# Two groups of 32 nodes, each in half of TensorE's columns, in a graph-attention kernel

## The chip, the cores and the metric

The kernel runs on one core of a Trainium2 chip. The metric is the device time of one execution in microseconds (us). Engines are named as in the profile: PE is TensorE's matmul stream, PEld its weight loads, DVE is VectorE, ACT is ScalarE, POOL is GpSimd and SP is SyncE; a "q" behind a name (SPq) is that engine's instruction queue, which issues transfers.

## The reference

The input is a graph of 6250 nodes with 128 features each and 106250 edges, sorted by destination. Two transformer convolutions with two heads run one after the other, with a batch norm and a ReLU between them, then a residual and a layer norm. All is float32. Cut to what matters:

```
def conv(h, edge_attr, src, dst, W...):          # H = 2 heads, C = 64
    q, k, v = h @ Wq + bq, h @ Wk + bk, h @ Wv + bv
    e = edge_attr @ We                           # edge_attr: 32 cosines of time, 64 given
    alpha = sum_c(q[dst] * (k[src] + e)) / sqrt(C)      # one score for each edge and head
    a = softmax of alpha over the edges of one dst
    return segment_sum((v[src] + e) * a, dst) + h @ Ws + bs
h = relu(batch_norm(conv1(x)))
out = layer_norm(x + conv2(h))
```

## The kernel before

**Plan.** The edges are cut into NC = 106 chunks of whole destination nodes, about 1003 edges and at most NN = 64 nodes each. A chunk occupies CE = 1024 slots: T = 8 blocks of 128 edges, each block a tile with the edges on the partitions. A short stage (`tile_gnn_resnorm`) reads where the chunks begin (`nbs` the first node, `sls` the first edge), turns the edges' sources, destinations and times into columns (`columns`, into `srcs`, `dsts`, `ew`), and tests that the graph fits the scheme. The number of violations ends in `bad`, and the flag `oki` decides at run time between `ordered`, the code below, and `general`, a fallback. Every engine reads `oki`; on SyncE the last of the writes of the feature table `xv_d` stand behind that read.

**Tables.** For each node and head, the query is multiplied into the key matrix beforehand (`tables`), so that the score of an edge is a dot product of a row of the table `tab` with the features of the edge's source, plus one with the edge's own attributes. A code of the node number (`fcode` against bits in the edge's record) adds a huge value where the edge does not belong to the node. So one chunk's scores are a matrix of 128 rows (64 nodes x 2 heads) by 1024 slots, in which only the edges of a row's own node count.

**Rounds.** `conv` runs once for each convolution, over rounds k; each round works on several chunks in a pipeline, in an order written out by hand (`tc.manual_schedule()`):

- `fetch(k + 4)` and `gather(k + 4)`: attributes and table rows come by SyncE's transfers, the features of the edges' sources by eight indirect transfers of 128 rows from GpSimd (L748). Six chunk buffers `ff` are in rotation; one comes free when its chunk's sums are done.
- `score(k, 0)` and `score(k, 1)` (L817, L818): for each half of 512 slots two matmuls, of the source features `ft` and of the edge attributes `et`, into `fps`, two banks of PSUM. Between the halves stands `turn_weights(k - 1)`.
- `lowest(k)` and `weigh(k)` (L823, L830): the minimum of each row on VectorE, the exponent on ScalarE, both over 1024 columns.
- `turn_weights(k - 1)` (L840, L841): the weights are transposed in eight blocks of 128 and copied to `fpt` by ScalarE.
- `turn_in(k + 1, u)` (L797, L806, L801, L807): features and, in the first convolution, attributes of the next chunk are transposed for the scores; ScalarE copies them to `fft` and `fet`.
- `divide`, `finish_turn`, `apply`, `finish` of chunk k - 2 (L852 to L895): the sums are divided by the sum of weights, transposed (`fat`) and multiplied by the value matrix. In the second convolution `apply` has a stationary operand of 64 columns (L883, L884).
- `extra` work, one or two steps in a round: tables of later nodes (L627) and rows of the result.
- `gather_sums(k - 1)` (L847), last in the round: eight matmuls, one for each block, whose stationary operand is a block of the transposed weights (128 slots x 128 rows) and whose moving operand is 225 columns of the block's features and attributes. They add up in one bank, `fpa`.

TensorE takes its instructions in the program's order, so the order above is that of its work. In the trace each float32 matmul of the program is two instructions with a weight load each (848 instructions for 424 calls of L817); a transpose is one.

Of the kernel before, what the change touches and what calls it, by code (L numbers as in the profile page):

```python
# [22 lines left out]
GE = GT * P  # L23
# [21 lines left out]
T = 8  # L45
CE = T * P
NN = P // H
NC = 106
EW = ED + 1

BITS = 8
EC = ED + 2 * BITS
# [482 lines left out]
def room(nc, pl, const, c, w):  # L535
# [38 lines left out]
def matrices(nc, pl, c, const, bank):  # L574
# [3 lines left out]
    for i, w in enumerate((wq, wk, web)):  # L578
# [82 lines left out]
def ordered(ctx: ExitStack, tc: tile.TileContext, pl, x, dst, edge_attr_64, conv2, bn_g, bn_b, out):  # L661


    nc = tc.nc
    N = x.shape[0]
    E = dst.shape[0]
    NP = pl.NP
    hT = pl.hT
    ident, wv, web, tw, tb = pl.ident, pl.wv, pl.web, pl.tw, pl.tb
# [18 lines left out]
    base = N - 2 * NN  # L688
# [10 lines left out]
    def conv(c, extra, first_blocks=None):  # L699
# [4 lines left out]
        work = cs.enter_context(tc.tile_pool(name=f"fwork{c}", bufs=2))  # L704
# [3 lines left out]
        p_s = cs.enter_context(tc.tile_pool(name=f"fp_s{c}", bufs=1, space=bass.MemoryType.PSUM))  # L708
# [10 lines left out]
        def fetch(k):  # L719
# [88 lines left out]
            if u:  # L808
                nc.sync.dma_start(et_d[k], s.et)

        def score(k, u):

            s = ch[k]
            if u == 0:
                s.ps = p_s.tile([P, CE], F32, name="fps")
            w = slice(u * GE, (u + 1) * GE)
            nc.tensor.matmul(s.ps[:, w], s.tab[:, :, 0], s.ft[:, w], start=True, stop=False)  # L817
            nc.tensor.matmul(s.ps[:, w], s.tab[:EC, :, 1], s.et[:, w], start=False, stop=True)  # L818

        def lowest(k):  # L820
            s = ch[k]
            low = small.tile([P, 1], F32, name="flow")
            nc.vector.tensor_reduce(low, s.ps, AX.X, OP.min)  # L823
            s.bias = small.tile([P, 1], F32, name="fm")
            nc.vector.tensor_scalar(s.bias, low, HIGHEST, None, op0=OP.min)  # L825

        def weigh(k):
            s = ch[k]
            s.s = work.tile([P, CE], F32, name="fs")
            nc.scalar.activation(s.s, s.ps, AF.Exp, bias=s.bias, scale=-1.0)  # L830

        def turn_weights(k):

            s = ch[k]
            s.pt = work.tile([P, CE], F32, name="fpt")
            for u in range(2):
                pp = p_tr.tile([P, GE], F32, name="fppt", tag="tr")
                for t in range(4):
                    at = u * GE + t * P
                    nc.tensor.transpose(pp[:, t * P:(t + 1) * P], s.s[:, at:at + P], ident)  # L840
                nc.scalar.copy(s.pt[:, u * GE:(u + 1) * GE], pp)  # L841

        def gather_sums(k):
            s = ch[k]
            s.pa = p_a.tile([P, D + EW], F32, name="fpa")
            for t in range(T):
                nc.tensor.matmul(s.pa, s.pt[:, t * P:(t + 1) * P], s.f[:, t, 1:1 + D + EW], start=t == 0, stop=t == T - 1)  # L847

        def divide(k):
            s = ch[k]  # L850
# [80 lines left out]
        with cs, tc.manual_schedule():  # L931
            for k in range(-AHEAD, NC + 3):
                def on(j):
                    return 0 <= j < NC

                if on(k + AHEAD):
                    fetch(k + AHEAD)
                    gather(k + AHEAD)
                if k == -AHEAD and c:
                    first_blocks()  # L940
                if on(k):
                    score(k, 0)
                if on(k - 1):
                    turn_weights(k - 1)
                place()
                if on(k - 2):
                    divide(k - 2)
                if on(k):
                    score(k, 1)
                if on(k - 2):  # L950
                    finish_turn(k - 2)
                if on(k):
                    lowest(k)
                if on(k + 1):
                    turn_in(k + 1, 0)
                if on(k - 2):
                    apply(k - 2)
                if on(k):
                    weigh(k)
                if on(k + 1):  # L960
                    turn_in(k + 1, 1)
                if on(k - 2):
                    finish(k - 2)
                for j in (k + 2,) if k < SINGLE else (k + 2, k + 3) if k == SINGLE else (k + 3,):
                    if c == 0 and on(j):
                        encode(j)
                        if j < SINGLE + 3:
                            sine()
                if k >= 0:
                    at_round[0] = k  # L970
                    pull(extra, 2 if k < 4 or k > 96 else 1)
                if len(args) == 3 or args and k == NC - 4:
                    sine()
                if c and on(k):
                    if k < RAW:
                        normalise(k)
                    nc.vector.tensor_copy(ch[k].f[:, :, 1 + D:1 + D + TD], ch[k].z)
                for _ in range(min(len(done), 2 if k > NC - 12 else 1)):
# [12 lines left out]
    with tc.tile_pool(name="fpw", bufs=2) as pw:  # L991
# [62 lines left out]
        scale = pl.scale = const.tile([P, 1], F32, name="fscale")  # L1054
# [68 lines left out]
def tile_gnn_resnorm(ctx: ExitStack, tc: tile.TileContext, x, src, dst, edge_attr_64, edge_weight, node_vec,  # L1123
                     time_w, time_b, conv1, conv2, bn_g, bn_b, out):
    nc = tc.nc
    N = x.shape[0]
    E = src.shape[0]
    step = -(-E // NC)
    keep = ctx.enter_context(tc.tile_pool(name="keep", bufs=1))
    made = ctx.enter_context(tc.tile_pool(name="made", bufs=1, space=bass.MemoryType.DRAM))  # L1130

# [5 lines left out]
    with tc.tile_pool(name="plan", bufs=1) as pl, tc.tile_pool(name="planw", bufs=2) as mw, \  # L1137
            tc.tile_pool(name="planp", bufs=2, space=bass.MemoryType.PSUM) as pp, tc.manual_schedule():
        R = NC - 1
        win = pl.tile([R, P], I32, name="win")  # L1140
        for r0, r1 in ((0, R // 16 * 16), (R // 16 * 16, R)):
            nc.sync.dma_start(win[r0:r1], bass.AP(tensor=dst.tensor, offset=dst.offset + step * (r0 + 1) - (P - 1),
                                                  ap=[[step, r1 - r0], [1, P]]))
        NP = got.NP = -(-(N + NN) // GE) * GE
        got.hT = keep.tile([P, NP], F32, name="fhT")
# [19 lines left out]
        jpp = pl.tile([P, P], I32, name="fjp")  # L1165
        nc.gpsimd.iota(jpp, pattern=[[1, P]], base=0, channel_multiplier=-1)
        tau_i = pl.tile([P, 1], I32, name="tau_i")
        nc.gpsimd.iota(tau_i, pattern=[[0, 1]], base=step, channel_multiplier=step)
        lane_i = pl.tile([P, 1], I32, name="lane_i")
        nc.gpsimd.iota(lane_i, pattern=[[0, 1]], base=0, channel_multiplier=1)  # L1170
        ident = got.ident = keep.tile([P, P], F32, name="fident")
# [5 lines left out]
        ends = pl.tile([1, 2, NC + 1], F32, name="ends")  # L1177
# [55 lines left out]
        bad = pl.tile([1, 4], F32, name="bad")  # L1233
        nc.vector.tensor_scalar(bad[:, 3:], ends[:, 0, NC - 2:NC - 1], N - NN + 0.5, None, op0=OP.is_gt)
        nc.vector.tensor_reduce(bad[:, 0:1], span, AX.XY, OP.add)

        two = pl.tile([1, NC - 1], F32, name="two")
# [49 lines left out]
        pb = pp.tile([1, 1], F32, name="pb", tag="one", bufs=1)  # L1287
        nc.tensor.matmul(pb, worst, ones[:, 0:1], start=True, stop=True)
        nc.vector.tensor_copy(bad[:, 1:2], pb)
        tot = pl.tile([1, 1], F32, name="tot")  # L1290
        nc.vector.tensor_reduce(tot, bad, AX.X, OP.add)
        nc.vector.tensor_scalar(oki, tot, 0.0, None, op0=OP.is_equal)
        columns(flats[1], dsts)
        columns(flats[2], ew)

    got.nbs, got.sls = nbs, sls
# [36 lines left out]
```

## Time and profile before

| | |
|---|---|
| median of 14 runs | 2283.13 us (2282.22 to 2286.94) |
| the profiled execution | 2286.03 us |
| its span | 2284.2 us |
| mean granted clock of TensorE | 0.985 |
| first convolution's gathers, first to last start | 37.4 to 1129.0 us |
| second convolution's gathers, first to last start | 1180.6 to 2245.9 us |
| DMA | 396.59 MB, mean 174 GB/s |

The profile is of one execution. Each line of a group shows source line, engine, operation and tiles (written <- read), partitions x elements, the number of instructions, their busy time and mean duration, and the idle time of the engine just ahead of them with what ended it ("issue" where the profile shows no other cause). A timeline line is start, duration, engine, line, operation, and in brackets the idle time before it. The chain of waits is followed back from the last instruction of the program, and its durations reach from one link to the next. Matmuls overlap in the array and their ends are modelled, so for TensorE the distance between starts says more than the durations.

### The profile page before, as it was taken

The numbers are of one execution on the slowest core, as the hardware profiler recorded it, in microseconds if no ns is written. First come the engines' busy times: TensorE is split into PE (matmuls) and PEld (weight loads), VectorE is DVE, ScalarE is ACT, GpSimd is POOL, SyncE is SP. The second block draws the span as 40 slices with busy tenths as digits, with TensorE's granted clock in tenths as the row PEclk, the third lists the DMA queues.
The fourth block names the chain that finished last, engine by engine and source line by source line (L and its number), as shares of the span: only waits on it lengthen the run. The fifth ranks groups of instructions, "written<-read, shape, count | busy, mean of one in ns | idle before, by whom it ended". The sixth has DMA issues, their size and how long they took to land.

```text
span 2284.2 us, 39277 instructions
## 1 busy us (share of the span) xinstructions
PE 2204.6 (97%) x11586; PEld 1705.0 (75%) x11586; DVE 1228.1 (54%) x3738; ACT 1225.4 (54%) x1955; POOL 1623.9 (71%) x1717
## 2 busy tenths in 40 slices
PE   5999999999999999999978999999999999999997
PEld 3687888778787888888855777777777777777775
DVE  5576767676676667777735433333433343433333
ACT  3677777766566666555643344444444444444444
POOL 3777777767777777777527777777777777777772
PEclk8999999999999999999988999999999999999999
DMA  7666666656666666666639666676666766666661
GB/s 236 171 187 164 179 186 182 182 147 181 185 178 170 170 188 177 176 175 170 159 97 245 178 183 171 178 188 184 182 180 171 190 177 183 183 168 164 164 155 40
DMA packets 431116, 396.59 MB, mean 174 GB/s; under 512 B 279697, under 2 KB 375182, under 8 KB 427566
## 3 DMA queue, kind: packets, MB, share of 16 engines
q1 hardware_dynamic: 357680, 239.73, 38.4%
q0 software_dynamic: 54656, 113.07, 20.8%
q10 hardware_dynamic: 18558, 41.20, 5.2%
q8 instruction: 95, 1.56, 0.3%
q14 instruction: 127, 1.04, 0.1%
HBM read 277.19 MB, written 113.17 MB: 171 GB/s over the span
## 4 chain that ended last, share of the span: by engine, by line
PE 72%; DVE 3%; DMA 2%; issue 1%; ACT 0%; SPq 0%; POOL 0%; ACTq 0%; DVEq 0%; POOLq 0%
PE fpa L847 23%; PE fps L817 13%; PE fps L818 13%; PE fppt L840 6%; PE fpx L797 5%; PE fpg L627 3%; PE fpe L806 2%; PE fpo L883 2%; DVE fat L870 2%; PE fpo L884 1%; PE fpo L868 1%; PE fpo L867 1%; PE fpo L877 1%; PE fpo L878 1%; DMA hn_d<-fhr 1%
## 5 line engine op out<-in xcount | busy, mean ns | idle before, releaser
L748 POOL DMA_INDIRECT ff<-xv_d,fsrcs x848 | 814.1, 960 | 304.8 <-issue 224.9
L748 POOL DMA_INDIRECT ff<-hn_d,fsrcs x824 | 782.1, 949 | 254.2 <-issue 219.1
L847 PE MATMUL fpa<-ff,fpt 128*128 128x225 f32 x3392 | 682.1, 354 | 0.0
L847 PEld LDWEIGHTS fpa<-ff,fpt 128*128 128x128 f32 x3392 | 635.5, 190 | 52.5 <-issue 48.6
L841 ACT COPY fpt<-fppt 128x512 f32<-128x512 f32 x424 | 228.1, 590 | 447.5 <-PE fppt L840 437.0
L817 PE MATMUL fps<-fft,ftab 128*128 128x512 f32 x848 | 443.0, 604 | 1.6 <-ACT fs L830 1.6
L801 ACT COPY fft<-fpx 128x512 f32<-128x512 f32 x418 | 242.9, 581 | 358.7 <-PE fpx L797 358.7
L870 DVE COPY fat<-fpo 128x256 f32<-128x256 f32 x212 | 90.0, 425 | 595.6 <-PE fpo L868 589.8
L830 ACT ACTIVATE fs<-fps,fm 128x1024 f32<-128x1024 f32 x212 | 236.2, 1114 | 81.6 <-DVE fm L825 70.7
L840 PEld LDWEIGHTS fppt<-fident,fs 128*128 128x128 f32 x1696 | 198.4, 140 | 104.8 <-issue 103.9
L797 PE MATMUL fpx<-fident,ff 128*128 128x128 f32 x1696 | 264.2, 279 | 10.8 <-ACT fo L631 6.8
L823 DVE TENSOR_REDUCE flow<-fps 128x1 f32<-128x1024 f32 x212 | 257.5, 1215 | 8.5 <-PE fps L818 8.5
L840 PE MATMUL fppt<-fident,fs 128*128 128x128 f32 x1696 | 220.1, 272 | 0.0
L818 PE MATMUL fps<-fxT,ftab 112*128 112x512 f32 x424 | 217.7, 594 | 1.3 <-DMA fxT<-et_d 1.3
L818 PE MATMUL fps<-fet,ftab 112*128 112x512 f32 x424 | 218.0, 595 | 0.0
L797 PEld LDWEIGHTS fpx<-fident,ff 128*128 128x128 f32 x1696 | 195.5, 142 | 22.7 <-ACT fo L631 8.6
L817 PEld LDWEIGHTS fps<-fft,ftab 128*128 128x128 f32 x848 | 166.5, 226 | 5.4 <-ACT fs L830 3.3
L818 PEld LDWEIGHTS fps<-fet,ftab 112*128 112x128 f32 x424 | 106.5, 251 | 76.1 <-issue 59.8
L818 PEld LDWEIGHTS fps<-fxT,ftab 112*128 112x128 f32 x424 | 83.8, 198 | 100.8 <-issue 97.5
L852 DVE TENSOR_SCALAR finv<-fpa 128x1 f32<-128x1 f32 x212 | 32.2, 152 | 211.1 <-issue 97.4
L772 DVE SCALAR_TENSOR_TENSOR farg<-fturns,farg 128x256 f32<-128x256 f32 x318 | 135.3, 426 | 10.9
L806 PE MATMUL fpe<-fident,ff 128*112 128x128 f32 x848 | 129.2, 276 | 1.6 <-DVE ff L784 1.4
(202 smaller groups left out, 2320.9 us busy)
## 6 DMA issues: line engine op xcount, KB each, us to landing
ff<-in_edge_attr SPq DMA_DIRECT2D x212, 256.0 KB
et_d<-fet SPq DMA_DIRECT2D x106, 448.0 KB
fxT<-et_d SPq DMA_DIRECT2D x106, 448.0 KB
ftab<-tab_d SPq DMA_DIRECT2D x106, 192.0 KB
tab_d<-fo ACTq DMA_DIRECT2D x13, 1536.0 KB
ff<-xv_d,fsrcs POOLq DMA_INDIRECT x848
enc_d<-fzs SPq DMA_DIRECT2D x106, 128.0 KB
ftab<-tab_d SPq DMA_DIRECT2D x106, 128.0 KB
```

What stands on the lines that cost most here:

```text
L748: nc.gpsimd.indirect_dma_start(out=f[:, t, (1 if c else 0):1 + D], out_offset=None, in_=(h_d if k < RAW else hn_d) if c else pl.xv_d, in_o ...
L797: nc.tensor.transpose(px[:, t * P:(t + 1) * P], s.f[:, u * 4 + t, 1:1 + D], ident)
L801: nc.scalar.copy(s.ft[:, u * GE:(u + 1) * GE], px)
L806: nc.tensor.transpose(pe[:EC, t * P:(t + 1) * P], s.f[:, u * 4 + t, 1 + D:], ident)
L817: nc.tensor.matmul(s.ps[:, w], s.tab[:, :, 0], s.ft[:, w], start=True, stop=False)
L818: nc.tensor.matmul(s.ps[:, w], s.tab[:EC, :, 1], s.et[:, w], start=False, stop=True)
L823: nc.vector.tensor_reduce(low, s.ps, AX.X, OP.min)
L830: nc.scalar.activation(s.s, s.ps, AF.Exp, bias=s.bias, scale=-1.0)
L840: nc.tensor.transpose(pp[:, t * P:(t + 1) * P], s.s[:, at:at + P], ident)
L841: nc.scalar.copy(s.pt[:, u * GE:(u + 1) * GE], pp)
L847: nc.tensor.matmul(s.pa, s.pt[:, t * P:(t + 1) * P], s.f[:, t, 1:1 + D + EW], start=t == 0, stop=t == T - 1)
L870: nc.vector.tensor_copy(s.at, s.po)
```

## The change

The 64 nodes of a chunk become two groups of 32. With two heads a group has 64 rows, and it takes 64 columns of TensorE: the first group's products go to PSUM partitions 0 to 63, the second's to 64 to 127. Since edges are sorted by destination, the first group's edges lie at the front of the chunk's slots and the second's at the back. Each group is computed over WT = 5 blocks, WE = 640 slots: the first over slots 0 to 639, the second over 384 to 1023.

- Scores: for 512 and then 128 slots, two matmuls for each group, so eight calls with 64 stationary columns instead of four with 128. All of them stand at the start of the round; `score(k, 1)` is gone.
- Minimum, exponent and transposed weights cover 640 columns instead of 1024; five transposes instead of eight, copied as 512 and 128 columns.
- Sums: five blocks for each group, ten calls with 64 stationary columns instead of eight with 128.
- Plan: a new test sees that the group border of every chunk lies between slots 384 and 640. It needs `dsts`, so `columns(flats[1], dsts)` is moved ahead of `oki`, with six more small VectorE operations. The chunks' beginnings are shifted by the 68 edges by which 106 x 1003 exceeds the number of edges.

The diff, cut to its core:

```diff
-        def score(k, u):
+        def score(k):
             s = ch[k]
-            if u == 0:
-                s.ps = p_s.tile([P, CE], F32, name="fps")
-            w = slice(u * GE, (u + 1) * GE)
-            nc.tensor.matmul(s.ps[:, w], s.tab[:, :, 0], s.ft[:, w], start=True, stop=False)
-            nc.tensor.matmul(s.ps[:, w], s.tab[:EC, :, 1], s.et[:, w], start=False, stop=True)
+            s.ps = p_s.tile([P, CE], F32, name="fps")
+            for lo, hi in ((0, GE), (GE, WE)):
+                for i, (tab, of) in enumerate(((s.tab, s.ft), (s.tab[:EC], s.et))):
+                    for g in range(2):
+                        at = g * (CE - WE)
+                        nc.tensor.matmul(s.ps[g * NN:(g + 1) * NN, lo:hi], tab[:, g * NN:(g + 1) * NN, i], of[:, at + lo:at + hi],
+                                         start=i == 0, stop=i == 1)
...
-            nc.vector.tensor_reduce(low, s.ps, AX.X, OP.min)
+            nc.vector.tensor_reduce(low, s.ps[:, :WE], AX.X, OP.min)
...
-            nc.scalar.activation(s.s, s.ps, AF.Exp, bias=s.bias, scale=-1.0)
+            nc.scalar.activation(s.s, s.ps[:, :WE], AF.Exp, bias=s.bias, scale=-1.0)
...
-            for u in range(2):
+            for lo, hi in ((0, GE), (GE, WE)):
                 pp = p_tr.tile([P, GE], F32, name="fppt", tag="tr")
-                for t in range(4):
-                    at = u * GE + t * P
-                    nc.tensor.transpose(pp[:, t * P:(t + 1) * P], s.s[:, at:at + P], ident)
-                nc.scalar.copy(s.pt[:, u * GE:(u + 1) * GE], pp)
+                for at in range(lo, hi, P):
+                    nc.tensor.transpose(pp[:, at - lo:at - lo + P], s.s[:, at:at + P], ident)
+                nc.scalar.copy(s.pt[:, lo:hi], pp[:, :hi - lo])
...
-            for t in range(T):
-                nc.tensor.matmul(s.pa, s.pt[:, t * P:(t + 1) * P], s.f[:, t, 1:1 + D + EW], start=t == 0, stop=t == T - 1)
+            for t in range(WT):
+                for g in range(2):
+                    nc.tensor.matmul(s.pa[g * NN:(g + 1) * NN], s.pt[:, t * P + g * NN:t * P + (g + 1) * NN],
+                                     s.f[:, t + g * (T - WT), 1:1 + D + EW], start=t == 0, stop=t == WT - 1)
...
                 if on(k):
-                    score(k, 0)
+                    score(k)
                 if on(k - 1):
                     turn_weights(k - 1)
                 place()
                 if on(k - 2):
                     divide(k - 2)
-                if on(k):
-                    score(k, 1)
...
         nc.vector.tensor_copy(bad[:, 1:2], pb)
+        columns(flats[1], dsts)
+        split = pl.tile([1, 3, NC], F32, name="split")
+        nc.vector.tensor_scalar(split[:, 0], ends[:, 0, :NC], NH - 0.5, None, op0=OP.add)
+        for i, (t, op) in enumerate(((T - WT, OP.is_gt), (WT, OP.is_lt))):
+            nc.vector.tensor_copy(split[:, 1 + i], dsts[0:1, t])
+            nc.vector.tensor_tensor(split[:, 1 + i], split[:, 1 + i], split[:, 0], op)
+        nc.vector.tensor_reduce(bad[:, 4:], split[:, 1:], AX.XY, OP.add)
         tot = pl.tile([1, 1], F32, name="tot")
         nc.vector.tensor_reduce(tot, bad, AX.X, OP.add)
         nc.vector.tensor_scalar(oki, tot, 0.0, None, op0=OP.is_equal)
-        columns(flats[1], dsts)
         columns(flats[2], ew)
```

More of the change, by code (lines that the diff above doesn't have):

```diff
@@ L49 @@
 EW = ED + 1
+WT = 5
+WE = WT * P
+NH = NN // 2
 BITS = 8
@@ L828, in weigh @@
             s = ch[k]
-            s.s = work.tile([P, CE], F32, name="fs")
-            nc.scalar.activation(s.s, s.ps, AF.Exp, bias=s.bias, scale=-1.0)
+            s.s = work.tile([P, WE], F32, name="fs")
+            nc.scalar.activation(s.s, s.ps[:, :WE], AF.Exp, bias=s.bias, scale=-1.0)
         def turn_weights(k):
             s = ch[k]
-            s.pt = work.tile([P, CE], F32, name="fpt")
-            for u in range(2):
+            s.pt = work.tile([P, WE], F32, name="fpt")
+            for lo, hi in ((0, GE), (GE, WE)):
                 pp = p_tr.tile([P, GE], F32, name="fppt", tag="tr")
-                for t in range(4):
-                    at = u * GE + t * P
-                    nc.tensor.transpose(pp[:, t * P:(t + 1) * P], s.s[:, at:at + P], ident)
-                nc.scalar.copy(s.pt[:, u * GE:(u + 1) * GE], pp)
+                for at in range(lo, hi, P):
+                    nc.tensor.transpose(pp[:, at - lo:at - lo + P], s.s[:, at:at + P], ident)
+                nc.scalar.copy(s.pt[:, lo:hi], pp[:, :hi - lo])
         def gather_sums(k):
@@ L1128, in tile_gnn_resnorm @@
     step = -(-E // NC)
+    less = NC * step - E
     keep = ctx.enter_context(tc.tile_pool(name="keep", bufs=1))
@@ L1141, in tile_gnn_resnorm @@
         for r0, r1 in ((0, R // 16 * 16), (R // 16 * 16, R)):
-            nc.sync.dma_start(win[r0:r1], bass.AP(tensor=dst.tensor, offset=dst.offset + step * (r0 + 1) - (P - 1),
+            nc.sync.dma_start(win[r0:r1], bass.AP(tensor=dst.tensor, offset=dst.offset + step * (r0 + 1) - less - (P - 1),
                                                   ap=[[step, r1 - r0], [1, P]]))
@@ L1167, in tile_gnn_resnorm @@
         tau_i = pl.tile([P, 1], I32, name="tau_i")
-        nc.gpsimd.iota(tau_i, pattern=[[0, 1]], base=step, channel_multiplier=step)
+        nc.gpsimd.iota(tau_i, pattern=[[0, 1]], base=step - less, channel_multiplier=step)
         lane_i = pl.tile([P, 1], I32, name="lane_i")
@@ L1232, in tile_gnn_resnorm @@
         nc.vector.tensor_scalar(span[:, 1], span[:, 1], float(CE), None, op0=OP.is_gt)
-        bad = pl.tile([1, 4], F32, name="bad")
-        nc.vector.tensor_scalar(bad[:, 3:], ends[:, 0, NC - 2:NC - 1], N - NN + 0.5, None, op0=OP.is_gt)
+        bad = pl.tile([1, 5], F32, name="bad")
+        nc.vector.tensor_scalar(bad[:, 3:4], ends[:, 0, NC - 2:NC - 1], N - NN + 0.5, None, op0=OP.is_gt)
         nc.vector.tensor_reduce(bad[:, 0:1], span, AX.XY, OP.add)
```

## The prediction

> **What bounds the kernel now.** I read, in this order, the share of busy time, the costliest groups, the chain that ended last, and the timelines of GpSimd and TensorE. First the engines' busy time and the groups in question:
>
> ```profile
> PE 2204.6 (97%) x11586; PEld 1705.0 (75%) x11586; DVE 1228.1 (54%) x3738; ACT 1225.4 (54%) x1955; POOL 1623.9 (71%) x1717
> ```
> ```profile
> L748 POOL DMA_INDIRECT ff<-xv_d,fsrcs x848 | 814.1, 960 | 304.8 <-issue 224.9
> L847 PE MATMUL fpa<-ff,fpt 128*128 128x225 f32 x3392 | 682.1, 354 | 0.0
> L817 PE MATMUL fps<-fft,ftab 128*128 128x512 f32 x848 | 443.0, 604 | 1.6 <-ACT fs L830 1.6
> ```
>
> TensorE looks like the only bound, but look at GpSimd's gathers: each is 0.96 us long and is followed by 0.30 us. The timeline shows the 0.30 even where nothing is late:
>
> ```profile
> 1600.11 0.94 POOL L748 DMA_INDIRECT ff<-hn_d,fsrcs  x1 [0.30 <-issue]
> 1601.36 0.94 POOL L748 DMA_INDIRECT ff<-hn_d,fsrcs  x1 [0.30 <-issue]
> ...
> 1128.97 0.94 POOL L748 DMA_INDIRECT ff<-xv_d,fsrcs  x1 [0.30 <-issue]
> 1180.61 0.94 POOL L748 DMA_INDIRECT ff<-h_d,fsrcs  x1 [50.70 <-ACT fhT L1089]
> ...
> 2245.85 0.94 POOL L748 DMA_INDIRECT ff<-hn_d,fsrcs  x1 [0.30 <-issue]
> ```
>
> So eight gathers, one chunk, can't take less than 8 x (0.960 + 0.30) = 10.1 us in the first convolution and 8 x (0.949 + 0.30) = 10.0 us in the second. TensorE's rounds, from the starts of the sums in the chain: 61 rounds from 526.99 to 1153.35 us, 10.27 us each; 97 rounds from 1242.32 to 2200.55 us, 9.88 us each. The two engines are level. One round of the first convolution in the chain:
>
> ```profile
> 673.46 3.04 PE fpa L847 x16
> 676.50 0.86 PE fps L817 x2
> 677.36 0.86 PE fps L818 x2
> 678.22 0.88 PE fppt L840 x8
> 679.09 0.92 PE fps L817 x2
> 680.01 0.86 PE fps L818 x2
> ```
>
> Sums, scores and weight transposes take 3.04 + 3.50 + 0.88 = 7.42 us. Who waits for whom is in the answer for the gathers' line (total us, times):
>
> ```profile
>   PE fpa L847: 43.1, 76
> ```
>
> Less the 0.30 that each gather has anyway, GpSimd waited 43.1 - 76 x 0.30 = 20.3 us for TensorE to release chunks, all in the first convolution. In the second it waited for TensorE nowhere.
>
> **Scores and sums.** A matmul of the program is two instructions, and its time goes by the moving columns: 0.86 us for 512, 0.22 for 128 (L877, L878), 0.38 for 225. Scores go from four matmuls of 512 columns to four of 512 and four of 128; sums from eight to ten; weight transposes from eight to five at 0.11.
> - If the two halves of the array work one after the other: 4 x 0.86 + 4 x 0.22 = 4.32, 10 x 0.38 = 3.80, 5 x 0.11 = 0.55; together 8.67, or +1.25 us a chunk.
> - If they work side by side: half of that for scores and sums, plus one instruction of stagger, since a group's two instructions follow each other on its half: 2.16 + 0.43, 1.90 + 0.19, and 0.55; together 5.23, or -2.19 us.
>
> **Change of tiling.** The second convolution already has a 64-column product (L883, L884), so the trace shows what going in and out costs:
>
> ```profile
> 1610.73 0.34 PE L883 MATMUL fpo<-fwv,fat 128*64 128x64 f32 x2
> 1610.85 0.20 PEld L884 LDWEIGHTS fpo<-fwe,fat 128*64 128x64 f32 x2
> 1611.15 0.28 PE L884 MATMUL fpo<-fwe,fat 128*64 128x64 f32 x2
> 1611.36 0.42 PEld L797 LDWEIGHTS fpx<-fident,ff 128*128 128x128 f32 x4
> 1611.36 0.66 PE L797 MATMUL fpx<-fident,ff 128*128 128x128 f32 x4
> ```
>
> Inside the stretch pairs start 0.12 apart. The next pair would have been due at 1611.27, it starts at 1611.36, its load with it and not ahead of it, and that costs another 0.06: 0.15 us out. I take the same in. Sums and the following scores share one stretch, so it is twice a chunk: +0.3 us. Totals: **-1.9 us** a chunk side by side, **+1.55** in series. No row shows two column halves at once. I take side by side: in the built kernel the groups stand at columns 0 and 64 and write different PSUM partitions, so nothing in the program orders them, and the trace shows TensorE loading weights beside a running matmul for 75% of the span. Series stays as an end.
>
> [...] The trace: L884's load starts at 1610.85, beside L883's second matmul, on the same 128 rows; loads are hidden there. [...]
>
> **Order.** All score matmuls now stand ahead of the weight transposes. What this moves up is the need for the second half of `fft` and `fet`: its two ScalarE copies (0.58 and 0.59) were covered by sums, half the scores and transposes, now by the sums alone, about 2.1 us. `fat`'s transposes L867 come after 3.1 us of cover instead of 5.3; the divide they need takes 0.9 (L852 to L855). Neither comes due, and with the gathers as pace a late copy eats slack. ScalarE's exponent and VectorE's minimum shrink from 1024 to 640 columns (1.11 and 1.22 us; about 0.4 and 0.45 less, an estimate by columns): hidden in the loop, on the path only at the ends.
>
> **Start.** The flag `oki` now waits for the transposed `dsts` and six more small operations; SyncE issues its last table write behind that flag:
>
> ```profile
> 28.88 0.14 DVE L1292 TENSOR_SCALAR oki<-tot 1x1 int32<-1x1 f32 x1
> ```
> ```profile
> 30.55 0.33 SPq L529 DMA_DIRECT2D xv_d<-fxrows  x1
> ```
>
> Cast to end of the two copies is 28.95 to 31.47, 2.5 us; eight small operations in a row (L1230 to L1240) took 2.0. So the flag comes at 28.7 + 2.5 + 2.0 = 33.2 instead of 29.0. Queued behind it on SyncE are that write, the rest's, three loads and the first chunk's fetch; every gather waits for the writes. +4.2 us, fully exposed.
>
> **Where it ends.** Side by side, TensorE needs 8.4 and 8.0 us a round, below the gathers' 10.1 and 10.0, so the gathers set the pace throughout and most of the 1.9 us becomes idle time of TensorE.
> - The 20.3 us of waiting vanish.
> - After the last gather of the first convolution (1128.97) TensorE is behind: its last sums start at 1167.93, 39.0 us later. In the second, where it has caught up, 2245.85 to 2268.69, 22.8 us. The lag of 16.2 us vanishes.
> - Both tails are run through with shorter work: two sums and one set of scores, transposes, minimum and exponent: 0.95 x 2 + 0.9 + 0.35 + 0.45 + 0.4 = 4.0 us, twice 8.0.
> - The start adds 4.2.
>
> 20.3 + 16.2 + 8.0 - 4.2 = 40.3 us. The profiled execution took 2286.0 us (span 2284.2), 2.9 above the median of 2283.1; the difference is applied to the median: **2243 us**.
>
> **Rivals.**
> - *The halves don't overlap.* TensorE then paces both convolutions: 106 x 1.55 = 164 us in the first, about 161 in the second (it ran behind the gathers there until 2214 us), plus 4: 2612 us; without the tiling cost 2550. For it: no row shows overlap. It decides where less than 1.55/(1.55 + 1.9) = 45% of the overlap comes. Chance 15%.
> - *Part of the overlap*, because a group's loads or first matmul wait for the other's: at a third +0.4 us a chunk, 2283 + 85 + 4 = 2372; from 2290 to 2450, 7%. At about half the gain of the waits pays for the start: no change, 4%.
> - *The gathers are no floor.* Their 0.960 in the first convolution against a usual 0.944 may be disturbance by a busier chip: 848 x 0.016 = 13.6 us more, 2229. This lies in my main case, as does the tail that doesn't shrink (2259).
> - *The new test fails* and the fallback runs. Excluded from the reference's seeded edges: at slot 384 the node is at most the 27th of its chunk, at slot 640 at least the 36th; the border is between 32 and 33.
>
> **Numbers.** Main case 74%, with a range of its own of 2228 to 2260; no change 4%; slower 22%. To hold 8 in 10 the range takes in the no-change case and most of the partial one: 2226 to 2400. Under 0.2% (4.6 us) no measurement here tells a change from none. Faster 0.74, same 0.04, slower 0.22.
>
> **What would show it.** Right: matmuls of the two groups start well under 0.43 us (scores) and 0.19 us (sums) apart in pairs, sums take about 2.1 us a chunk and scores 2.6; GpSimd stands at 1.25 us a gather with no wait for L847's successor; TensorE's busy share falls towards 80%; the pause between the convolutions falls from 51 to about 31 us; the first gather starts near 41.6. Wrong: twenty sums instructions 0.19 apart one after another, 3.8 us, and rounds over 11 us.

## The result, and the profile after

The changed kernel takes 2253.72 us (median of 6 runs, 2248.08 to 2254.36) beside 2283.64 us of the kernel before on the same chip: ratio 0.9863, 95% interval 0.9853 to 0.9872. That is 29.9 us less, where 40 were predicted (2243 us). The profiled execution took 2252.37 us, its span is 2250.6 us. On a second chip the same kernel took 2254.12 us, ratio 0.9871 (0.9855 to 0.9888).

First the busy time and the groups of the page:

```profile
PE 1865.8 (83%) x13494; PEld 1258.5 (56%) x13494; DVE 1151.4 (51%) x3744; ACT 1095.8 (49%) x1955; POOL 1623.0 (72%) x1717
```
```profile
L752 POOL DMA_INDIRECT ff<-xv_d,fsrcs x848 | 813.9, 960 | 287.3 <-issue 205.7
L853 PE MATMUL fpa<-ff,fpt 128*64 128x225 f32 x4240 | 497.8, 385 | 0.0
L801 PE MATMUL fpx<-fident,ff 128*128 128x128 f32 x1696 | 336.0, 305 | 152.3 <-DMA ff<-hn_d,fsrcs 139.9
L874 PE MATMUL fpo<-fident,fa 128*128 128x128 f32 x212 | 64.4, 304 | 158.1 <-DVE fa L862 158.1
```

The gathers take what they took (0.960 us each); TensorE has become idle for 17% of the span. Its two largest idle times stand ahead of the transposes of the divided sums (L874), which wait for VectorE's divide, and ahead of `turn_in` (L801), which now waits for a gather's data. Next, one round of the first convolution in TensorE's timeline (start, duration, engine, line, operation):

```profile
650.81 2.12 PE L853 MATMUL fpa<-ff,fpt 128*64 128x225 f32 x20
652.76 1.03 PE L823 MATMUL fps<-fft,ftab 128*64 128x512 f32 x4
653.62 1.03 PE L823 MATMUL fps<-fet,ftab 112*64 112x512 f32 x4
654.48 0.39 PE L823 MATMUL fps<-fft,ftab 128*64 128x128 f32 x4
654.70 0.39 PE L823 MATMUL fps<-fet,ftab 112*64 112x128 f32 x4
655.02 0.76 PE L845 MATMUL fppt<-fident,fs 128*128 128x128 f32 x5
655.62 0.27 PE L874 MATMUL fpo<-fident,fa 128*128 128x128 f32 x1
```

Twenty sums instructions go by in 1.95 us, one every 0.19 us for each of the two halves; scores take 2.26 us, transposes 0.60. Together 4.81 us a chunk (650.81 to 655.62), where the kernel before took 7.42. In the single records of this round the two groups' sums and scores start in pairs, 6 to 10 ns apart. Now GpSimd's timeline at the border of the convolutions, and what the gathers' line waited for in the whole span (total us, times):

```profile
1111.49 0.94 POOL L752 DMA_INDIRECT ff<-xv_d,fsrcs  x1 [0.30 <-issue]
1152.70 0.94 POOL L752 DMA_INDIRECT ff<-h_d,fsrcs  x1 [40.26 <-ACT fhT L1094]
```
```profile
  issue: 434.5, 1426
  ACT fhT L1094: 40.3, 1
...
  PE fpx L801: 20.4, 67
```

Sums (L853) are no longer among the causes, and 67 waits of 20.4 us are just the 0.30 that every gather has. The span splits at the gathers (starts, from the trace):

| stretch | before, us | after, us | change | predicted |
|---|---|---|---|---|
| start to first gather | 37.4 | 39.9 | +2.5 | +4.2 |
| first convolution, first to last gather | 1091.6 | 1071.6 | -20.0 | -20.3 |
| pause to the second one's first gather | 51.6 | 41.2 | -10.4 | -20.2 |
| second convolution, first to last gather | 1065.2 | 1065.6 | +0.3 | 0 |
| last gather to end | 38.4 | 32.3 | -6.1 | -4.0 |

The predicted 20.2 of the pause is its lag of 16.2 and one tail of 4.0. The changes add up to the spans' 33.6 us, rounded. In the profile from the second chip the changed kernel's first stretch is 1075.7 us and its pause 40.8, so single terms of the table are good to some 4 us.

### The profile page after: what moved, and what is told of

The parts are those of the page before. It is cut to its first block, busy times and chain, and to the rows that moved or that the text cites. A ratio compares the mean times of both kernels' runs of the same rounds, so it can differ in the third digit from the quotient of the medians.

```text
span 2250.6 us, 43133 instructions
## 1 busy us (share of the span) xinstructions
PE 1865.8 (83%) x13494; PEld 1258.5 (56%) x13494; DVE 1151.4 (51%) x3744; ACT 1095.8 (49%) x1955; POOL 1623.0 (72%) x1717
## 4 chain that ended last, share of the span: by engine, by line
POOL 16%; PE 15%; DMA 14%; issue 9%; DVE 4%; ACT 1%; SPq 0%; POOLq 0%; DVEq 0%; ACTq 0%
POOL ff L752 16%; DMA ff<-hn_d,fsrcs 10%; PE fpa L853 5%; PE fps L823 4%; PE fpx L801 2%; DMA ff<-xv_d,fsrcs 1%; PE fppt L845 1%; PE fpg L631 1%; DMA hn_d<-fhr 1%; DVE farg L776 1%; DMA ftab<-tab_d 0%; PE fpg L1080 0%; PE fpo L890 0%; DMA fxT<-et_d 0%; DVE farg L770 0%
## 5 line engine op out<-in xcount | busy, mean ns | idle before, releaser
L853 PE MATMUL fpa<-ff,fpt 128*64 128x225 f32 x4240 | 497.8, 385 | 0.0
L801 PE MATMUL fpx<-fident,ff 128*128 128x128 f32 x1696 | 336.0, 305 | 152.3 <-DMA ff<-hn_d,fsrcs 139.9
L853 PEld LDWEIGHTS fpa<-ff,fpt 128*64 128x64 f32 x4240 | 310.3, 148 | 203.2 <-issue 93.9
L846 ACT COPY fpt<-fppt 128x512 f32<-128x512 f32 (+1 forms) x424 | 159.9, 429 | 531.5 <-PE fppt L845 520.2
L801 PEld LDWEIGHTS fpx<-fident,ff 128*128 128x128 f32 x1696 | 224.2, 152 | 208.0 <-DMA ff<-hn_d,fsrcs 166.7
L823 PE MATMUL fps<-fft,ftab 128*64 128x512 f32 (+1 forms) x1696 | 310.6, 437 | 2.2 <-DMA ftab<-tab_d 2.0
L877 DVE COPY fat<-fpo 128x256 f32<-128x256 f32 x212 | 90.0, 425 | 298.8 <-PE fpo L875 286.7
L823 PEld LDWEIGHTS fps<-fft,ftab 128*64 128x64 f32 x1696 | 139.7, 154 | 139.2 <-issue 114.2
L874 PE MATMUL fpo<-fident,fa 128*128 128x128 f32 x212 | 64.4, 304 | 158.1 <-DVE fa L862 158.1
L836 ACT ACTIVATE fs<-fps,fm 128x640 f32<-128x640 f32 x212 | 169.1, 798 | 24.2 <-DVE fm L831 22.4
L829 DVE TENSOR_REDUCE flow<-fps 128x1 f32<-128x640 f32 x212 | 172.7, 815 | 7.5 <-PE fps L823 7.5
L859 DVE TENSOR_SCALAR finv<-fpa 128x1 f32<-128x1 f32 x212 | 32.1, 152 | 276.8 <-issue 198.5
L823 PE MATMUL fps<-fxT,ftab 112*64 112x512 f32 (+1 forms) x848 | 152.8, 436 | 2.1 <-DMA fxT<-et_d 2.1
L823 PE MATMUL fps<-fet,ftab 112*64 112x512 f32 (+1 forms) x848 | 153.4, 432 | 0.0
L811 ACT COPY fet<-fpe 112x512 f32<-112x512 f32 x212 | 126.7, 598 | 9.0 <-PE fpe L810 8.6
```

The lines of the kernel that those rows point to most:

```text
L801: nc.tensor.transpose(px[:, t * P:(t + 1) * P], s.f[:, u * 4 + t, 1:1 + D], ident)
L811: nc.scalar.copy(s.et[:, u * GE:(u + 1) * GE], pe[:EC])
L823: nc.tensor.matmul(s.ps[g * NN:(g + 1) * NN, lo:hi], tab[:, g * NN:(g + 1) * NN, i], of[:, at + lo:at + hi], start=i == 0, stop=i == 1)
L829: nc.vector.tensor_reduce(low, s.ps[:, :WE], AX.X, OP.min)
L836: nc.scalar.activation(s.s, s.ps[:, :WE], AF.Exp, bias=s.bias, scale=-1.0)
L846: nc.scalar.copy(s.pt[:, lo:hi], pp[:, :hi - lo])
```

## Experiments

Theory: the two column halves work at the same time; that puts TensorE's round below the gathers', and from there the gathers alone set the pace. Rivals: the gain comes from fewer slots and not from the halves; or TensorE still sets the pace. Every ratio below is against the kernel before on the same chip.

### No overlap at all: both groups in the same half

```diff
-nc.tensor.matmul(s.ps[g * NN:(g + 1) * NN, lo:hi], ..., start=i == 0, stop=i == 1)
+nc.tensor.matmul(s.ps[:NN, lo:hi], ..., start=i == 0 and g == 0, stop=i == 1 and g == 1)
-nc.tensor.matmul(s.pa[g * NN:(g + 1) * NN], ..., start=t == 0, stop=t == WT - 1)
+nc.tensor.matmul(s.pa[:NN], ..., start=t == 0 and g == 0, stop=t == WT - 1 and g == 1)
```

`ps` and `pa` are allocated and filled with ones once, ahead of the rounds.

> Both groups in columns 0 to 63 of TensorE, in the same alternating order, so that nothing can run side by side; both groups' scores and sums add up in PSUM partitions 0 to 63, partitions 64 to 127 hold ones written once, so the values are not the reference's. Theory (the gain comes from the two column halves): scores 4.3, sums 3.8 us a chunk, with some 3.0 and 2.5 us of other TensorE work and 0.2 for the switch rounds of 11.9 and 11.3 us in place of the gathers' 10.1 and 10.0, and a lag at the end of the first convolution: 2254 + 190 + 132 + 15 = about 2590 us, 2540 to 2640 (1.11 to 1.16 of before). Rival (the gain comes from fewer columns, from 1024 to 640, and the hardware hides the rest whatever the columns): like the order in series, about 2265 us.

Measured: 2601.66 us, ratio 1.1391 (1.1372 to 1.1410). Its timeline of TensorE, the same part of a round, and the gathers' group with what ended their idle time:

```profile
650.01 4.01 PE L856 MATMUL fpa<-ff,fpt 128*64 128x225 f32 x20
653.87 1.88 PE L826 MATMUL fps<-fft,ftab 128*64 128x512 f32 x4
...
658.27 0.76 PE L848 MATMUL fppt<-fident,fs 128*128 128x128 f32 x5
```
```profile
L755 POOL DMA_INDIRECT ff<-xv_d,fsrcs x848 | 805.0, 949 | 461.8 <-issue 224.2 <-PE fpa L856 203.1 <-DMA fwv<-in_L_gnn_Wv 28.4
```

Same instructions, same order, same columns of data: sums 3.86 us, scores 4.40, rounds of 11.89 and 11.45 us (means of 80 and 75 rounds), and GpSimd waits 203 us for the sums in the first convolution alone. Fewer slots without the halves cost 316 us; the halves are the whole gain. Overlap is worth (3.86 + 4.40) / (1.95 + 2.26) = 1.96 times.

### The same halves, one group after the other

```diff
-for lo, hi in ((0, GE), (GE, WE)):
-    for i, (tab, of) in ...:
-        for g in range(2):
+for g in range(2):
+    for lo, hi in ((0, GE), (GE, WE)):
+        for i, (tab, of) in ...:
...
-for t in range(WT):
-    for g in range(2):
+for g in range(2):
+    for t in range(WT):
```

> All instructions of the first group ahead of all of the second, for scores and sums. Theory (the gain comes from two column halves at work at the same time, which needs the two groups' instructions to alternate in TensorE's queue): per chunk scores go back from 2.3 to about 4.3 us and sums from 1.95 to about 3.8, rounds of 8.2 become about 12, TensorE is busy throughout and the time is 2540 to 2640 us (1.11 to 1.16) on a usual chip. Rival (the queue looks far enough ahead, or fewer columns alone do it): within 1% of the changed kernel.

Measured: 2265.32 us, ratio 0.9921 (0.9905 to 0.9938). The theory's 300 us more did not come. The rival's number did: 11 us, or 0.5%, above the changed kernel's 2254.12 on the same chip. Its reason holds in part, as the timeline shows:

```profile
654.50 2.74 PE L853 MATMUL fpa<-ff,fpt 128*64 128x225 f32 x17
656.90 0.68 PE L823 MATMUL fps<-fft,ftab 128*64 128x512 f32 x1
657.08 0.54 PE L853 MATMUL fpa<-ff,fpt 128*64 128x225 f32 x2
...
661.64 0.27 PE L874 MATMUL fpo<-fident,fa 128*128 128x128 f32 x1
```

Sums and scores are interleaved in time though they are not in the program. In the single records of this round six sums instructions start 0.19 us apart, alone; then, 5 ns after the seventh, a second train of ten begins beside it, with the same spacing. It is so in all 212 rounds. The eleventh instruction in program order is the first of the other half, so it started while three of the first half still waited. At the border from the second group's sums to the first group's scores it is the same, and there the line numbers show it: the first score (L823, 656.90) starts ahead of the last three sums (L853, from 657.08). So 7.14 us a chunk (654.50 to 661.64): of the 8.87 us without overlap (650.01 to 658.88 in the kernel above) less 4.81 with it, 1.73 of 4.06, or 43%, is won by this order too. And 7.14 is 0.28 below the 7.42 of before, just enough for TensorE to keep up with the gathers: their first stretch is 1075.9 us, beside 1075.7 in the changed kernel on the same chip. What remains is mostly the end of the first convolution: the pause is 48.3 us against 40.8.

### More TensorE work

```diff
+for g in range(2):
+    at = g * (CE - WE)
+    nc.tensor.matmul(s.ps[g * NN:(g + 1) * NN, :GE], s.tab[:, g * NN:(g + 1) * NN, 0], s.ft[:, at:at + GE], start=True, stop=True)
```

> The first pair of score matmuls (512 columns, both groups) is computed twice: 0.86 us more of TensorE in each of the 212 rounds. Theory (the gathers set the pace, TensorE idles some 1.7 us a round): only the two ends and the rounds with the longest VectorE wait grow, 2 to 12 us in all, 1.000 to 1.005 of the changed kernel. Rival (TensorE still sets the pace, its idle time is only waits inside its own chain): up to 212 x 0.86 = 182 us more, near 2430 us.

Measured: 2254.70 us, ratio 0.9877 (0.9860 to 0.9893), beside 2254.12 of the changed kernel on the same chip. The page's busy line:

```profile
PE 1968.0 (87%) x14342; PEld 1282.6 (57%) x14342; DVE 1151.8 (51%) x3744; ACT 1095.5 (49%) x1955; POOL 1627.6 (72%) x1717
```

TensorE is busy for 102 us more and the time stays: the gathers' stretches are within 2.1 us of the changed kernel's on the same chip, and only the pause grew, by 2.3 us. TensorE is not the bound. The products done twice are 212 x 0.86 = 182 us; the busy time grew by less because less of it ran at half clock, 155 us in place of 309 by the trace's record of the granted clock (see the last section).

### One gather fewer, in both kernels

```diff
+table = (h_d if k < RAW else hn_d) if c else pl.xv_d
+nc.sync.dma_start(f[:, T - 1, (1 if c else 0):1 + D], table[:P, :])
-for t in range(T):
+for t in range(T - 1):
     nc.gpsimd.indirect_dma_start(...)
```

> The changed kernel with seven indirect gathers a chunk; block 7's rows come by one plain SyncE transfer of the table's first 128 rows, so its features are not those of the edges' sources. Theory (the gathers are the floor, TensorE needs 8.0 to 8.4 us a round): floor 7 x 1.26 = 8.84 and 7 x 1.25 = 8.75 us a round, both stretches shrink by about 133 us, near 1990 us; up to 2060 (0.87 to 0.90) if VectorE's waits for the gathers stretch rounds. Rival (TensorE's idle time is inside its own chain of waits, which sets the pace as well): above 2200 us.

> The kernel before with the same seven gathers and one plain transfer. Theory (TensorE stood level with the gathers there): its rounds of 10.27 and 9.88 us stay, so the first stretch keeps its time and the second loses at most 106 x 0.16 = 17 us: 2262 to 2284 us, 0.990 to 1.000. Rival (the gathers alone were the bound of the kernel before, and TensorE only filled the time they left): as much less as in the changed kernel, near 2030 us.

Measured: the changed kernel 2001.97 us, ratio 0.8759 (0.8744 to 0.8775); the kernel before 2278.74 us, 0.9973 (0.9963 to 0.9983). The gathers' groups of the two, first the changed kernel's:

```profile
L754 POOL DMA_INDIRECT ff<-xv_d,fsrcs x742 | 719.5, 970 | 258.9 <-issue 174.9 <-DVE fbits L735 28.7 <-DMA ff<-xv_d,fsrcs 17.9
```
```profile
L750 POOL DMA_INDIRECT ff<-xv_d,fsrcs x742 | 711.2, 959 | 398.7 <-issue 181.4 <-PE fpa L849 80.8 <-DMA ff<-xv_d,fsrcs 66.3
```

The same relief brings 252 us to the one and 7 to the other, where GpSimd's waits for the sums (L849) rise to 81 us in the first convolution alone. So before, TensorE held the pace within a few us of the gathers; after, only the gathers do, down to rounds of 9.07 and 8.74 us at least (by the estimate 7 x 1.26 and 7 x 1.25, seven gathers need 8.8). With seven gathers the change would be worth 277 us instead of 30.

### The sums alone

```diff
 # score, lowest, weigh, turn_weights as in the kernel before, over CE slots
+for t in range(WT):
+    for g in range(2):
+        u = t + g * (T - WT)
+        nc.tensor.matmul(s.pa[g * NN:(g + 1) * NN], s.pt[:, u * P + g * NN:u * P + (g + 1) * NN],
+                         s.f[:, u, 1:1 + D + EW], start=t == 0, stop=t == WT - 1)
```

> The sums alone in two groups of 64 columns; scores, minimum, exponent and weight transposes over 1024 slots as before. Theory (what counts is only that TensorE's round falls below the gathers'): sums 1.95 us and 0.2 for the switch in place of 3.04, so 6.5 in place of 7.42 a chunk, rounds of 9.4 and 9.0 us, below 10.1 and 10.0: GpSimd's waits for TensorE vanish as in the full change, and only the ends are longer, as in the order in series: 2260 to 2268 us, 0.990 to 0.993. Rival (each part pays by its share of TensorE's time): 0.9 of 2.6 us, a third of the 30 us: 2272 to 2276 us, 0.995 to 0.997.

Measured: 2257.03 us, ratio 0.9885 (0.9868 to 0.9901), even below what was expected. One round of its timeline:

```profile
657.40 2.12 PE L852 MATMUL fpa<-ff,fpt 128*64 128x225 f32 x20
659.45 1.19 PE L821 MATMUL fps<-fft,ftab 128*128 128x512 f32 x2
```

The sums with the way out of the tiling take 2.05 us, for 3.04 before. This 1.0 of the 2.6 us that TensorE saves in the full change brings 24.8 us of the 30: the gain is not proportional to TensorE's time, it ends where the round falls below the gathers'.

### Why the pause shrank by half of what was predicted

The chain of waits of the changed kernel (start, us to the next link, what) after the last gather of the first convolution:

```profile
1111.49 2.35 DMA ff<-xv_d,fsrcs
...
1114.19 0.18 DVE frel L769
...
1118.54 0.17 DVE finv L859
...
1118.93 0.46 DVE fa L862
...
1119.53 0.30 PE fpo L874
...
1122.13 2.05 PE fpa L853 x20
```

`divide` (L859 to L862) works on sums that were done 2.4 us before (they started at 1114.06 and took 2.12). It stands on VectorE's queue behind the encoding (L769 to L777) of the chunk three rounds ahead, whose last gather has only now landed; behind the divide, TensorE's transposes (L874) and everything after them wait. In the whole span this is `PE fpo L874 <- DVE fa L862`, 158.1 us in 82 waits, longest 9.1; in the kernel before it was 5.8 us in 5. From round 40 on (`SINGLE`) each chunk is encoded three rounds ahead, with one sine call for two chunks; up to there it is two rounds ahead and a sine call each. So when the last gather lands, the divides of older chunks still stand behind its encoding. The edit, with one that tests the border of each chunk on its own partition, ahead of the transposes:

```diff
-SINGLE = 40
+SINGLE = NC
...
+nc.tensor.matmul(pn[:NC], ends[:, 0, :NC], ones[0:1, 0:1], start=True, stop=True)
+nc.vector.tensor_scalar(edge[:NC], pn[:NC], NH - 0.5, None, op0=OP.add)
+for i, (t, op) in enumerate(((T - WT, OP.is_gt), (WT, OP.is_lt))):
+    nc.vector.tensor_copy(side[:NC, i:i + 1], flats[1][:NC, t, 0:1])
+    nc.vector.tensor_tensor(side[:NC, i:i + 1], side[:NC, i:i + 1], edge[:NC], op)
+    nc.vector.tensor_add(worst[:NC], worst[:NC], side[:NC, i:i + 1])
...
-columns(flats[1], dsts)        # and the six operations of split
 nc.vector.tensor_scalar(oki, tot, 0.0, None, op0=OP.is_equal)
+columns(flats[1], dsts)
```

> Two edits: every chunk is encoded by itself two rounds ahead in all rounds, in place of pairs three rounds ahead from round 40 on, so that the divide on VectorE does not queue behind an encode that waits for the newest gather; and the border test works on one chunk per partition before the transposes, so that the flag does not wait for the transposed destinations. Theory: first gather 2.5 us earlier, the pause between the convolutions shrinks from 41 to between 31 and 36 us; 2238 to 2248 us, 0.980 to 0.985 of before on a usual chip. Rival (the doubled sine calls and table loads on ScalarE, 1.28 us each, come due in the second half of the first convolution): 53 rounds that each grow by up to 1 us, slower than the changed kernel by 10 to 50 us.

Measured: 2248.97 us, ratio 0.9848 (0.9831 to 0.9865), 5 us below the changed kernel on the same chip, whose interval overlaps, and a microsecond above the expected range. GpSimd's timeline at the border:

```profile
1114.03 0.95 POOL L752 DMA_INDIRECT ff<-xv_d,fsrcs  x1 [0.30 <-issue]
1149.23 0.94 POOL L752 DMA_INDIRECT ff<-h_d,fsrcs  x1 [34.25 <-ACT fhT L1094]
```

The pause is 35.2 us, 6.0 shorter than in the first profile and 5.6 than in the same chip's. In the changed kernel five sets of sums start after the last gather, 2.6, 10.6, 18.2, 24.6 and 29.3 us behind it; here it is four, at 3.2, 12.3, 18.9 and 23.6. One round fewer is left, which is what moving the encoding by one round should do, and the doubled sine calls cost nothing (the first stretch is 1074.4 us beside 1075.7). The waits for the divide are not gone: in the whole span they are 163.9 us in 97, longest 6.1. What counts is where in the order the encoding stands. The start, however, gained only 0.3 us of 2.5. Of each timeline, SyncE's write and the copy it releases, first the changed kernel's:

```profile
33.48 0.33 SPq L533 DMA_DIRECT2D xv_d<-fxrows  x1
37.48 1.03 ACT L657 COPY fxT<-fpx 128x512 f32<-128x512 f32 x1 [9.11 <-DMA xv_d<-fxrows]
```
```profile
30.55 0.32 SPq L533 DMA_DIRECT2D xv_d<-fxrows  x1
37.02 1.02 ACT L657 COPY fxT<-fpx 128x512 f32<-128x512 f32 x1 [7.75 <-DMA xv_d<-fxrows]
```

The flag came 3.5 us earlier and the write was issued 2.9 earlier, but what waits for the table's writes started only 0.5 us earlier. From that write to the first gather it took 9.1 us in this execution, 6.3 to 6.9 in the profiles of the kernel before and of the changed one. The early test alone, in the profile from the chip of the next section, has its first gather at 37.8 us, beside 39.8 to 40.8 of the three variants without it there: the test can bring the first gather forward by 2 to 3 us. What held the writes here is not settled.

### Four runs on a chip that cannot answer

The first four variants ran on a chip where the kernel before took 2830.97 us, a quarter more than elsewhere. Each was expected as follows.

The groups one after the other, as above:

> The changed kernel with the loops turned: all score matmuls of group 0, then all of group 1, and the same for the sums. The same 18 calls a chunk on the same data; only neighbours in the order no longer stand on different halves. Theory A (what pays is that two neighbouring calls run side by side on the two column halves): TensorE needs 8.67 + 0.2 us a chunk for scores, sums and weight transposes instead of 4.9, rounds of 11 to 12 us, sums about 3.8 us a chunk, time 2550 to 2615 us. Rival B (what pays is less work: fewer transposes, fewer slots, shorter weight loads): 2250 to 2260 us, sums near 2 us.

The sums alone, where the second group's sums take the weights of blocks 0 to 4 in place of 3 to 7:

> Scores, minimum, exponent and weight transposes over 1024 columns and 128 rows as in the kernel before; only the sums are in two groups. TensorE saves 3.04 - 1.95 - 0.2 = 0.9 us a chunk instead of 2.5. Theory A (the eight gathers of a chunk are the floor, 10.0 to 10.1 us, and anything below it is enough): rounds of 9.4 and 9.0 us of work are still below the floor, so nearly all of the gain stays: 2250 to 2268 us, no wait of GpSimd for TensorE. Rival B (the time follows TensorE's work): 0.9/2.5 of the 30 us, that is about 2273 us or more.

The first edit of the last experiment alone, and its second alone:

> The changed kernel with the time encoding done one chunk at a time, for chunk k + 2 in every round, instead of chunk k + 3 from round 40 on with one sine for two chunks. Theory A (from round 40 on VectorE's queue holds the encoding of chunk k + 3, which waits for the newest gather, ahead of the divide of an older chunk, so TensorE is held a round behind the gathers): last gather to last sums of the first convolution shrinks from 29 us by about one round of 7 us, time about 2246 us. Rival B (the tail is long because TensorE's granted clock is low there, 0.80, or the rounds are simply that long): 29 us stay, 2254 us. Rival C: the ScalarE table loads, two of 1.28 us more in every second round, hold the exponent back: 2254 us or slower.

> The changed kernel with the new test of the group border made early, with chunks on the partitions and added to the violations that are counted anyway, so that the flag no longer waits for the transposed destinations. Theory A (the flag's delay is fully on the path of the first gather): first gather back from 39.9 to about 37.4 us, time 2.5 us less, about 2251 us. Rival B (the delay is hidden by the first rounds, which wait for other things): no change, 2254 us.

Measured: 2998.56 us, ratio 1.0594 (1.0541 to 1.0647); 2841.77, 1.0049 (1.0021 to 1.0077); 3049.52, 1.0792 (1.0751 to 1.0834); 3019.23, 1.0682 (1.0636 to 1.0728). Three are slower than the kernel before by 6 to 8%, the sums alone by 0.5%, and the expectations' sums do not apply there: in the last one's profile the instructions take what they take elsewhere (gathers 955 ns, sums 398), but engines that wait for TensorE start late. The waits of `fat`'s copy (L877), the changed kernel's on the first chip, and the fourth variant's here ("remote" is the profile's word for another core or an unknown queue):

```profile
DVE fat L877 <- PE fpo L875: 286.7, 206, 3.0
```
```profile
DVE fat L877 <- remote: 454.5, 83, 9.8
```

On the first chip this copy starts 36 to 39 ns after the modelled end of the transpose before it, in all 212 cases; here the median is 1.56 us and one in twenty takes 5 us. There GpSimd waits for the sums again, 681 us in all. That TensorE's rounds are drawn out by waits for such copies, which its saved work doesn't shorten, is argued and not tested. What delays the hand-over there is open: neither the kernel before nor the changed one was profiled on that chip. The same edits, or kernels that contain them, were run again elsewhere and are told of above.

## Why the prediction was right, and where its terms were off

- **The bound.** Right: the gathers are the floor, 10.1 and 10.0 us a chunk, and the kernel stands on it. The extra TensorE work that cost 0.6 us, and the 252 against 7 us of one gather fewer, show it.
- **Side by side.** Right. The rival "the halves don't overlap" gave 2612 us, or 2550 without the cost of the tiling; the kernel without overlap took 2601.66. Its estimate for the work in series, 8.67 us a chunk or 8.97 with the tiling, measured 8.87 with it. Within the main case the stagger of 0.43 and 0.19 us does not exist: a pair starts within 10 ns, and the saving is 2.6 us a chunk and not 1.9. It changed nothing, since TensorE's surplus was idle already.
- **Partial overlap** was given the decisive point of 45%. The order in series has 43% and is faster by 0.8%. By the measured terms the point lies at (8.87 - 7.42) / 4.06 = 36%, and since both engines had been level, a quarter of a microsecond was enough.
- **The loads.** Hidden, as in the prediction's row of L884: in every kernel here loads stand on the same 112 or 128 rows, in the kernel without overlap on the same columns too, and instructions of 225 columns still follow each other every 0.19 us, loads of some 0.14 us beside them.
- **The waits of 20.3 us.** Right: the gathers no longer wait for sums, and that stretch is 20.0 us shorter. That it agrees to 0.3 us is partly luck, since the stretch was 4 us longer on the second chip.
- **The lag of 16.2 us at the end of the first convolution, and its tail of 4.0.** This is the step that was mis-sized: 10.4 came in place of 20.2. It was assumed that TensorE, once caught up, ends as long after the last gather as in the second convolution. The last sums now start 29.3 us after it there and 15.3 in the second, so 14.0 of the lag of 16.2 are still there: five sets of sums are left behind the last gather of the first convolution, and three behind that of the second, before and after alike. So the lag is two more rounds to do, which a faster TensorE shortens and does not remove: the pause shrank because each round left became shorter (6.7 us in place of 8.6). One of the two rounds comes from the order: only the first convolution encodes, and VectorE's queue holds the divide behind the encoding of the newest gather. Encoding two rounds ahead leaves four sets and gives 6 of the missing 10 us back. What keeps the other is open.
- **The second tail.** 6.1 for 4.0: from last gather to last sums it shrank from 22.8 to 15.3 us.
- **The start.** +2.5 for +4.2. The flag came 3.5 us later, the write behind it 2.9 and the first gather 2.5: the added operations took less than assumed, and 1.0 us was made up on the way to the gather.
- **TensorE's busy share** is 83% and not 80%, because 309 us of its busy time ran at half clock (below); at full clock it would be 1865.8 - 309 / 2 = 1711 us, or 76%, an estimate.

-20.0 - 10.4 - 6.1 + 2.5 + 0.3 gives the 33.6 us of the spans against the predicted 40.3; the pause falls short by 9.8, and the start and the last stretch give 3.8 of it back.

## What to carry to other kernels

Two engines that stand level hide each other: relieve one and the gain ends at the other's pace, however much is saved, so work out the second engine's floor first, and look for the part of the change that just reaches it (here the sums alone). When a bound falls away, read in the timeline in what order the engines that had slack do their work: an operation that waits for the newest data, ahead of one that doesn't, was the next wait at the end here (the divide, behind the encoding, 2.4 us after its sums were done). Matmuls of 64 columns each were worth their number here where they stood in different column halves and near each other in the program's order: 0.987 of the time before alternating, 0.992 one group after the other, 1.139 in the same half.

## What was not expected of the hardware

**The two halves start past each other.** With the groups in series, the first instruction of the other half started while three of the first half still waited, in sums (beside the seventh of ten, in all 212 rounds) and in scores (beside the fifth of eight). None started while more than three waited. So here, between the two halves, the program's order is not the order of the starts. In the kernel before the 208 rounds that have sums, scores, transposes and products all start them in the program's order.

**The granted clock is lower where TensorE idles.** Two of TensorE's groups in the second convolution of the changed kernel:

```profile
1601.45 0.48 PE L801 MATMUL fpx<-fident,ff 128*128 128x128 f32 x1 [3.82 <-DMA ff<-hn_d,fsrcs]
...
1605.74 3.25 PE L853 MATMUL fpa<-ff,fpt 128*64 128x225 f32 x20
1608.82 1.02 PE L823 MATMUL fps<-fft,ftab 128*64 128x512 f32 x4
```

After 3.82 us of idle time the same twenty sums instructions take 3.08 us in place of 1.95. In the single records their pairs start 0.37 us apart up to 1608.05 and 0.19 apart from 1608.25 on: half the clock at first, then all of it. The mean granted clock is 0.53 from 1601.0 to 1605.7 us, 0.62 from there to 1608.8, and 1.00 behind it; the trace's record of the clock has no value but 0.5 and 1. From first to last start, 183 of the 212 sets of sums took at most 2.5 us (the usual is 1.77) and 29 more; in the 5 us ahead TensorE had idled 0.60 us (median) before the first kind and 2.18 before the second. The mean granted clock follows: 0.914 where TensorE is busy for 83%, 0.957 with the extra work (87%), 0.973 with the sums alone (93%), 0.985 in the kernel before (97%). The page's rows of the granted clock, of the changed kernel and of the one in series:

```profile
PEclk7899999989989999999978999999999998999898
```
```profile
PEclk7999999999999999999989999999999999999999
```

Of the changed kernel's 73 stretches at half clock 46 last 3.41 us, and all but one of the others a multiple of it. In the 3.41 us ahead of one TensorE was busy for 39% (median), so a stretch does not take idle time throughout; what sets one off is not shown. The time lost stayed within TensorE's slack: the gathers' second stretch is 1065.6 us, beside 1065.2 before.
